# A four-stage transformer block on one core: unread products split around a branch, expert results by halves, and output pieces woven into the next stage

## The chip, the cores and the metric

The kernel runs on one core of a Trainium2 chip. The metric is the device time of one execution in microseconds (us), lower is better. The engines are named as the profile names them: PE (TensorE, matrix products), DVE (VectorE), ACT (ScalarE), POOL (GpSimd) and SP (SyncE, which here only issues DMAs).

## The reference

The inputs are `x` (4 batches of 512 tokens, 256 features, float32) and one condition vector per batch. Cut to its stages:

```python
moe  = sum over the 2 best of 8 experts: weight * (relu(relu(x@W1+b1)@W2+b2)@W3+b3)
x    = x + linear_attention(moe)         # 8 heads, blocks of 32, elu(q@proj)+1 features
c    = softmax_attention(x, condition)   # 16 heads of 16, coherence gate and field term
for layer in (0, 1):                     # local attention, 8 heads of 64, window 128
    c = c + local_attention(shift(c)) @ wo
    c = c + gated_gelu_mlp(layernorm(shift(c)))
out  = x + c
```

All arithmetic is float32. A product with 512 columns shows in the trace as two matmul records with two weight loads.

## The kernel before, in words

The program is one straight stream with one branch. Its stages follow each other, and each holds the four batches `b` as tiles of 128 tokens.

**Experts.** Each token goes to two experts. Tokens are gathered by expert into slots; each slot runs `layer`, `layer`, `last`, and `last` scatters its rows with an indirect DMA to the DRAM table `ys`. Two rare slots stand behind a runtime branch, `with tc.If(halves > NHALF - NRARE)` (L1460), which this input does not take. After the branch `busy(13)` issues 13 products of `xres[0]` that nobody reads (`pbusy`). Then, for each batch, two DMAs fetch `g` from `ys` (L1477), ACT scales the first (L1481) and DVE adds the second (L1482) into `y[b]` (`ymoe` in the trace).

**Linear attention** (`lin`). `front(b)` turns `y[b]` by PE transposes (`pt`) into `yT`, then makes `qk` and `v`. `features`, `scores` and `values` follow; `values` ends in a chain: ACT adds a small number to the sum `pz` (L1564), DVE takes its reciprocal (L1565), and DVE multiplies (L1566) into `aT`. `tail(b)` multiplies `aT` by `awo` (`pao`) and DVE adds it to `xres[b]` (L1576). One loop weaves the front of the next batch and the tail of the previous one between the products of this one.

**Conditioned attention** (`cond_stage`). `front(b)` transposes `xres[b]` into `xT2`, makes `qm` (`pcq`), `kT` (`pck`), values `v1` (`pcv`) and the gate (`pct` and small products). `attend` runs scores (`sc`), exponentials on ACT (`cex`) and values (`pv`), with fronts and tails of other batches as fill. `tail(b)` makes `yc[b]`.

**Local attention and MLP** (`local_stream`, two layers). `front` transposes `yc[b]` (`pdt`), projects it (`pdq`), and rotates q and k with DVE and POOL, with a table `tab` that DVE first scales.

**What sets the order.** Within `PE.in_order()` every PE instruction is pinned behind the one written just before it. All other instructions, on PE and on every other engine, are placed at build time by the framework's planner: it runs the program with its own costs, takes what it believes ready, and of several ready ones the one written first. So the order on DVE, ACT and POOL, and of unpinned PE work, is the planner's. At run time each engine follows its fixed list. Tiles are rotating buffers in pools; a pool that opens where another closed waits, address by address, for the last reader of the old tiles. [...] `lin` uses four for `mmt` tiles and four for `features`; `cond_stage` uses two for `mmt` (pool `ps1`) and six for scores (`sp`); `local_stream` uses all eight.

## Time and profile before

| | us |
|---|---|
| median of 3 runs | 1429.75 (1427.66 to 1430.11) |
| the profiled execution: its time | 1429.31 |
| its span, first to last instruction | 1427.5 |
| PE busy | 1354.0 (95%) |
| DVE busy | 667.0 (47%) |
| ACT busy | 586.0 (41%) |
| POOL busy | 230.4 (16%) |

The profiled execution lies 0.44 us under the median, and 1.8 us of its time lie outside the span. The granted PE clock was 0.981 of full speed over the span. The stages can be told apart by their tiles: experts up to 320.7 us, linear attention from 336.6 to 499.7, conditioned attention to 753, local attention and MLP to the end. "Idle before" names what released an engine; "issue" is a wait for nothing that the profile shows.

### The profile page before, as it was taken

The numbers are of one execution on the slowest core, as the hardware profiler recorded it, in microseconds if no ns is written. First come the engines' busy times: TensorE is split into PE (matmuls) and PEld (weight loads), VectorE is DVE, ScalarE is ACT, GpSimd is POOL, SyncE is SP. The second block draws the span as 40 slices with busy tenths as digits, with TensorE's granted clock in tenths as the row PEclk, the third lists the DMA queues.
The fourth block names the chain that finished last, engine by engine and source line by source line (L and its number), as shares of the span: only waits on it lengthen the run. The fifth ranks groups of instructions, "written<-read, shape, count | busy, mean of one in ns | idle before, by whom it ended". The sixth has DMA issues, their size and how long they took to land.

```text
span 1427.5 us, 19422 instructions
## 1 busy us (share of the span) xinstructions
PE 1354.0 (95%) x7624; PEld 835.6 (59%) x7624; DVE 667.0 (47%) x1297; ACT 586.0 (41%) x969; POOL 230.4 (16%) x219
## 2 busy tenths in 40 slices
PE   4999999998899799999999999999999999999998
PEld 3788888874566543333335555656655456556564
DVE  6222221223677642333226777754352767854331
ACT  3111111123555325554654647563222567474111
POOL 0324232111000020000102322100020312310010
PEclk8999999999999899999999999999999999999999
DMA  3577667623000000000111011211001010011000
GB/s 122 216 258 264 223 227 247 214 79 122 1 2 1 0 1 0 1 1 1 44 49 64 2 36 35 75 33 30 22 0 41 23 32 23 17 39 47 14 23 25
DMA packets 43645, 94.74 MB, mean 66 GB/s; under 512 B 9760, under 2 KB 25752, under 8 KB 40728
## 3 DMA queue, kind: packets, MB, share of 16 engines
q1 hardware_dynamic: 38984, 83.11, 17.6%
q0 software_dynamic: 3552, 9.70, 2.0%
q8 instruction: 63, 1.03, 0.3%
q10 hardware_dynamic: 1008, 0.58, 0.2%
q14 instruction: 38, 0.31, 0.1%
HBM read 84.08 MB, written 7.21 MB: 64 GB/s over the span
## 4 chain that ended last, share of the span: by engine, by line
PE 66%; DVE 5%; ACT 3%; issue 2%; DMA 1%; SPq 0%; DVEq 0%; POOL 0%; POOLq 0%
PE pdq L78 11%; PE pug L78 5%; PE sc L78 5%; PE pua L78 5%; PE pv L78 5%; PE pn L78 4%; PE pfy L78 4%; PE pdy L78 4%; PE pds L78 4%; PE pz L78 2%; PE pqt L82 2%; PE pqk L78 2%; PE pcq L78 1%; PE pur L78 1%; PE pcv L78 1%
## 5 line engine op out<-in xcount | busy, mean ns | idle before, releaser
L78 PE MATMUL pdq<-wqkv,yT 128*128 128x512 f32 x384 | 177.6, 603 | 4.5 <-ACT yT L583 4.5
L403 ACT ACTIVATE cex<-sc 128x1024 f32<-128x1024 f32 x128 | 124.1, 1021 | 95.8 <-PE sc L78 94.7
L78 PE MATMUL ph<-h,w 128*128 128x256 f32 (+1 forms) x704 | 133.4, 347 | 1.0 <-ACT h L1356 0.5
L653 DVE TENSOR_TENSOR p<-p,lmask 128x384 f32<-128x384 f32 (+1 forms) x128 | 98.4, 786 | 66.5 <-ACT p L651 65.0
L609 POOL TENSOR_TENSOR qr<-t,t 128x512 f32<-128x512 f32 x64 | 85.8, 1340 | 247.5 <-DVE t L606 229.8
L78 PEld LDWEIGHTS ph<-h,w 128*128 128x128 f32 x704 | 116.2, 191 | 13.3 <-DVE h L1358 0.7
L78 PEld LDWEIGHTS pdq<-wqkv,yT 128*128 128x128 f32 x384 | 69.5, 190 | 82.2 <-issue 72.8
L1358 DVE TENSOR_SCALAR h<-ph,w 128x256 f32<-128x256 f32 (+1 forms) x88 | 36.1, 438 | 164.5 <-PE ph L78 101.5
L1356 ACT ACTIVATE h<-ph,w 128x256 f32<-128x256 f32 (+1 forms) x88 | 35.4, 438 | 187.1 <-PE ph L78 132.5
L651 ACT ACTIVATE p<-pds,ss 128x256 f32<-128x256 f32 (+1 forms) x256 | 95.6, 457 | 35.8 <-PE pds L78 27.3
L78 PE MATMUL pug<-hT,w 128*128 128x512 f32 x160 | 78.3, 612 | 0.0
L599 ACT ACTIVATE sq<-pdq 128x512 f32<-128x512 f32 x64 | 38.3, 598 | 96.7 <-PE pdq L78 57.6
L78 PE MATMUL sc<-qm,kT 32*128 32x512 f32 x512 | 76.0, 647 | 0.0
L78 PE MATMUL pua<-hT,w 128*128 128x512 f32 x160 | 75.6, 595 | 0.0
L78 PE MATMUL pv<-cex,v 128*32 128x512 f32 x512 | 69.0, 604 | 1.7 <-DVE xT L292 1.7
L78 PE MATMUL ph<-xbT,w 128*128 128x256 f32 (+1 forms) x352 | 68.3, 346 | 0.0
L78 PE MATMUL po<-w,h 128*128 128x256 f32 x296 | 67.7, 380 | 0.5 <-ACT h L1356 0.5
L78 PE MATMUL pdy<-wo,oT 128*128 128x256 f32 x256 | 63.3, 392 | 3.3 <-DVE oT L693 3.3
L78 PE MATMUL pds<-qT,kT 64*128 64x256 f32 (+1 forms) x512 | 65.3, 375 | 0.0
L78 PEld LDWEIGHTS pds<-qT,kT 64*128 64x128 f32 x512 | 43.9, 186 | 32.9 <-issue 26.2
L78 PEld LDWEIGHTS ph<-xbT,w 128*128 128x128 f32 x352 | 58.4, 191 | 6.9 <-issue 0.9
L78 PE MATMUL pfy<-w,uA 128*128 128x256 f32 x256 | 61.2, 382 | 0.0
(294 smaller groups left out, 2103.5 us busy)
## 6 DMA issues: line engine op xcount, KB each, us to landing
w<-in_moe_w_dram SPq DMA_DIRECT2D x22, 1024.0 KB
w<-in_moe_w_dram SPq DMA_DIRECT2D x22, 640.0 KB
w<-in_moe_w_dram SPq DMA_DIRECT2D x22, 516.0 KB
zb<-rows SPq DMA_DIRECT2D x32, 256.0 KB
g<-ys SPq DMA_DIRECT2D x8, 512.0 KB
wqkv<-in_f_wqkv_dram SPq DMA_DIRECT2D x2, 1536.0 KB
w<-in_f_w_dram SPq DMA_DIRECT2D x2, 1408.0 KB
xres<-in_x_dram SPq DMA_DIRECT2D x4, 512.0 KB
```

The costliest lines, as they stand in the source:

```text
L78: cls._queue(nc.tensor.matmul(*args, **kw))
L82: cls._queue(nc.tensor.transpose(*args, **kw))
L403: nc.scalar.activation(ex, pss[j], AF.Exp, scale=CHD**-0.5)
L599: nc.scalar.activation(sq, p3, AF.Square)
L609: nc.gpsimd.tensor_tensor(qr_t[:, s], t1, t2, ALU.add)
L651: nc.scalar.activation(p[:, at], pss[r][:, at], AF.Exp, scale=d.ss[:, 2 * u + jj, 1, 2 * c + r : 2 * c + r + 1])
L653: nc.vector.tensor_tensor(p[:, :n], p[:, :n], lmask[:, :n], ALU.mult)
L1356: nc.scalar.activation(dst, src, AF.Relu, bias=bias)
L1358: nc.vector.tensor_scalar(dst, src, bias, 0.0, ALU.add, ALU.max)
```

## The change

It touches three places where one stage hands over to the next ("seams"), and moves work between them.

- **Experts to linear attention.** `busy(13)` behind the branch becomes `busy(3)` ahead of it and `busy(6)` behind it. Batch 0's results are fetched in four DMAs of half the size (two tiles of tokens each), batch 1's in two as before. Only batch 0 is summed at once; `weighted(b)` of the other batches is written at the head of their `front` in `lin`, and so are the DMAs of batches 2 and 3.
- **Linear to conditioned attention.** The last batch's `tail` is no longer run at the end of `lin`: it is handed to `cond_stage` as `before`, and its two output pieces are put, pinned, between pieces of `front(0)`: both transposes, both `pck`, then one output piece, one `pcq`, one output piece, one `pcq`. So that this works, `pck` now comes ahead of `pcq` in every `front`; batch 0's `xT2` and `kT` are written by ACT instead of DVE; `aT` of the last batch and `awo` live in the pool `wp` that stays open; the last reciprocal and product run in two halves; the score banks are allocated ahead of `ps1`; `v1` is cleared inside `front(0)` and `front(1)`.
- **Conditioned to local attention.** The first `front` of the first local layer is no longer pinned.

```diff
+    def cond_stage(W, cp, sp, safe, before=()):
...
-            v1s = []
-            for i in range(2):
-                v1 = cp.tile([128, NT, CH, 32], F32, tag=f"v1{i}", name=f"v1{i}", bufs=1)
-                nc.gpsimd.memset(v1, 0.0)
...
+        v1s = []
+
+        def make_v1():
+            i = len(v1s)
+            v1 = cp.tile([128, NT, CH, 32], F32, tag=f"v1{i}", name=f"v1{i}", bufs=1)
+            nc.gpsimd.memset(v1, 0.0)
+            nc.gpsimd.memset(v1[:, :, :, CHD : CHD + 1], 1.0)
+            v1s.append(v1)
...
-                nc.vector.tensor_copy(xT2[:, c, :], pt)
+                (nc.scalar.copy if b == 0 else nc.vector.tensor_copy)(xT2[:, c, :], pt)
...
+            if not safe and b < 2:
+                make_v1()
+            for c in range(2):
+                ps = mmt("pck")
+                mm(ps, [(W["wqkv"][:, k, H + c * 128 : H + (c + 1) * 128], xT2[:, k, :]) for k in range(2)])
+                if b == 0:
+                    nc.scalar.activation(kT[:, c, :], ps, AF.Identity, bias=col("bk", c))
+                else:
+                    nc.vector.tensor_scalar(kT[:, c, :], ps, col("bk", c), None, ALU.add)
+                yield
             for c in range(2):
                 ps = mmt("pcq")
...
-                ps = mmt("pck")
-                mm(ps, [(W["wqkv"][:, k, H + c * 128 : H + (c + 1) * 128], xT2[:, k, :]) for k in range(2)])
-                nc.vector.tensor_scalar(kT[:, c, :], ps, col("bk", c), None, ALU.add)
-                yield
...
-        run(front(0, ds[0]))
+        first = front(0, ds[0])
+        with PE.in_order():
+            for _ in range(4):
+                next(first)
+            for _ in before:
+                next(first)
+        run(first)
...
+        run(front(wa, 0, ds[0]))
         with PE.in_order():
-            run(front(wa, 0, ds[0]))
             for l in range(2):
...
-                "awo": lambda: weight("awo", [128, 2, H], chunks(a["a_woT"]), wl),
+                "awo": lambda: weight("awo", [128, 2, H], chunks(a["a_woT"]), wp),
...
             last(len(often) - 1, often[-1])
+
+            busy(3)
             with tc.If(halves > NHALF - NRARE):
...
-            busy(13)
...
-            for b in range(B):
-                gs = []
-                for k in range(2):
-                    g = gp.tile([128, NT, H], F32, tag=f"g{k}", name=f"g{k}", bufs=2)
-                    at = 1 + (k * B + b) * S
-                    nc.sync.dma_start(g, ys[at : at + S].rearrange("(t p) h -> p t h", p=128))
-                    gs.append(g)
+            busy(6)
+
+            def results(b):
+                gs = [gp.tile([128, NT, H], F32, tag=f"g{k}", name=f"g{k}", bufs=2) for k in range(2)]
+                n = 2 if b == 0 else NT
+                for t in range(0, NT, n):
+                    for k in range(2):
+                        at = 1 + (k * B + b) * S + t * 128
+                        nc.sync.dma_start(gs[k][:, t : t + n, :],
+                                          ys[at : at + n * 128].rearrange("(t p) h -> p t h", p=128))
+                return gs
+
+            def weighted(b, gs):
                 for t in range(NT):
...
+            both = {b: results(b) for b in range(2)}
+            weighted(0, both[0])
...
             def front(b, d):
+                if b:
+                    weighted(b, both[b])
+                if b + 2 < B:
+                    both[b + 2] = results(b + 2)
...
-                    d.aT = lp.tile([128, 2, S], F32, tag="aT", name="aT")
+                    pool, tag = (wp, "aTlast") if d is ds[-1] else (lp, "aT")
+                    d.aT = pool.tile([128, 2, S], F32, tag=tag, name="aT")
...
-                nc.vector.reciprocal(z, z)
-                nc.vector.tensor_tensor(d.aT[:, g, :], pn, z, ALU.mult)
+                n = S // 2 if d is ds[-1] and g == 1 else S
+                for at in range(0, S, n):
+                    half = slice(at, at + n)
+                    nc.vector.reciprocal(z[:, half], z[:, half])
+                    nc.vector.tensor_tensor(d.aT[:, g, half], pn[:, half], z[:, half], ALU.mult)
...
-            run(tail(B - 1, ds[B - 1]))
+            end = tail(B - 1, ds[B - 1])
...
+            sp = cst.enter_context(tc.tile_pool(name="sp", bufs=3, space=PSUM, reuse_waits="tile"))
             cst.enter_context(banks("ps1", mm=2))
-            sp = cst.enter_context(tc.tile_pool(name="sp", bufs=3, space=PSUM, reuse_waits="tile"))
...
-            y = cond_stage(cw_, cp, sp, False)
+            y = cond_stage(cw_, cp, sp, False, end)
```

More of the change, by code (lines that the diff above doesn't have):

```diff
@@ L271, in conditions @@
         W["csb"], W["faT"] = csb, faT
-    def cond_stage(W, cp, sp, safe):
+    def cond_stage(W, cp, sp, safe, before=()):
         csb, faT = W["csb"], W["faT"]
         y = [resp.tile([128, NT, H], F32, tag="res", name=f"yc{b}") for b in range(B)]
-        if not safe:
-            v1s = []
-            for i in range(2):
-                v1 = cp.tile([128, NT, CH, 32], F32, tag=f"v1{i}", name=f"v1{i}", bufs=1)
-                nc.gpsimd.memset(v1, 0.0)
-                nc.gpsimd.memset(v1[:, :, :, CHD : CHD + 1], 1.0)
-                v1s.append(v1)
+        v1s = []
[5 more added lines that the diff above has]
+            v1s.append(v1)
         def front(b, d):
```

## The prediction

> **What bounds the kernel now.** I read the page first (PE busy 95% of the span, granted clock 0.981), so only PE's idle time, PE's work that nobody reads, and PE at a lower clock can be won. The view of all waits of PE shows where the idle lies, and most of the long ones stand at the three seams. Busy time by stretch (columns: stretch, length, busy time and instructions of PE, weight loads, DVE, ACT, POOL; granted clock; DMA):

> ```profile
> 320.70:336.60 15.90, 12.52 (x26) 5.45 (x26) 3.77 (x9) 4.58 (x11) 1.19 (x3) 0.89 0.65 213
> 336.60:346.10 9.50, 7.12 (x20) 2.79 (x18) 5.95 (x9) 3.42 (x8) 2.57 (x1) 0.82 0.31 102
> 489.40:502.00 12.60, 7.48 (x26) 5.37 (x25) 6.18 (x6) 0.69 (x1) 2.23 (x2) 0.73 0.01 1
> 744.90:753.80 8.90, 6.36 (x38) 5.06 (x36) 4.46 (x10) 0.60 (x2) 0.23 (x2) 1.00 0.35 121
> ```

> The 12.52 us of the first row are all unread products. Three rows are also under full clock. The chain of waits at the first seam (start, length, what):

> ```profile
> 321.66 2.45 issue
> 324.11 12.23 PE pbusy L78 x24
> 336.34 0.81 ACT g L1481 x2
> ...
> 337.16 3.36 DVE ymoe L1482 x3
> ...
> 340.85 0.69 DVE yT L125
> ...
> 341.58 4.54 PE pqk L78 x6
> ```

> The timeline of the same time says that batch 0's sum is done long before the unread products end (ACT, then DVE, waiting for the DMA):

> ```profile
> 328.32 1.71 ACT L1481 ACTIVATE g<-g,m 128x256 f32<-128x256 f32 x4 [8.85 <-DMA g<-ys]
> 329.79 1.67 DVE L1482 SCALAR_TENSOR_TENSOR ymoe<-g,m,g 128x256 f32<-128x256 f32 x4 [8.59 <-DMA g<-ys]
> ```

> So `y[0]` is whole at 331.46, but its transposes stand behind `pbusy` until 337.04; then the copy of `yT`'s second half waits on DVE behind batch 2's sum. Second and third seam, from the chain:

> ```profile
> 490.19 3.37 DVE z L1565
> ...
> 494.40 5.33 PE pao L78 x12
> ...
> 500.58 0.64 PE pt L82 x4
> ```

> ```profile
> 745.73 0.67 PE pcot L82 x4
> ...
> 749.44 3.29 PE pcy L78 x14
> ...
> 753.84 17.45 PE pdq L78 x40
> ```

> At the second, PE idles 3.90 us for reciprocal and product, and the 12 output products then take 5.33 us where 8 took 1.73 earlier. At the third, PE waits in steps of 0.3 to 1.2 us for DVE copies.

> [...] after 3.4 us without products the clock is 0.50 from 325.5 to 328.5, and passes of `pbusy` come 0.855 us apart instead of 0.43; the same after the 3.90 us at 490.5 (0.53). [...] PE's record of the branch is at 320.5, its next instruction at 324.08, with no releaser.

> ```profile
> L1460 PEldq COMPARE_BRANCH x1: 358/358/358, 320.5 to 320.5; - x1
> ```

> [...] If PE's sequencer ran ahead, the branch would overlap queued products. The trace doesn't settle it: DVE's and ACT's branch records come 0.2 and 0.1 us after their last instruction's end, PE's when its last product runs.

> **First seam.** Removed: 7 of 13 unread products behind the branch net of 3 put ahead (14 passes go behind it, 6 come ahead). I take it that the branch follows the three: 320.5 + 6 x 0.43 = 323.1, plus the same 3.6 us, restart at 326.7. `busy(6)` is 12 passes: 5.2 us, or 6.2 if two us of them are at half clock; taken to 332.4. Four half-size DMAs carry the same bytes, so the last lands where batch 0's second did (329.75); only two sums of 0.48 are left: `y[0]` at 330.7, hidden under `busy(6)`. Eight transposes (1.04 us) to 333.4; ACT copies one half (0.59), DVE the other (0.68), to 334.2. Two `pqk` groups (4 passes, 1.72 us each) end at about 337.5, where before `features` began at 346.05: 8.5 us. Late next is DVE: POOL's `xres += bo` (2.57 us) waits for the last `pbusy`, since that reads `xres[0]`, and a DVE sum beside it took 2.57 us instead of 0.48 (the maximum of the L1482 row). It will now fall on batch 1's sum, which the planner may place ahead of the second `yT` copy: up to 2.5 us. I take half: **-7.5 us**. Bounds: -11 (the branch runs ahead, restart at 324.1, everything 2.6 earlier) and -5 (that, with POOL falling on batch 0's sum, or a second cold window of 1.7).

> **Sums in the next stream.** 12 ACT scalings (0.43, 5.1 us) and 12 DVE sums (0.42, 5.0 us) leave the seam. SP issues ten DMAs instead of eight (0.36 to 1.07 us each) with nothing else of its own until 707.6. Batch 2's rows can be asked for when batch 0's buffers are free (330.7), and before took 3.9 us for the first and 1.45 more for the second: there at 336, batch 3's by about 342, long before their transposes (before: past 390 and 425). From 380 to 470 DVE is busy 65.1 of 90 us and ACT 50.9, so there is room; but PE there waits 4.7 us for `f` and 3.2 for `sc`, so a sum placed ahead of these shows. **+0.5**, bounds 0 and +3.

> **Second seam.** Before, from the end of `pz` (489.36) to the first `pcv` (509.20): 19.84 us. After, PE's list is transposes 1.04, two `pck` 3.44, two `pcq` 3.44, two output pieces 3.46 at full clock: 11.4. The reciprocal (3.37, now 2 x 1.7) and product (2 x 0.36) end at 494.3 and lie under transposes and `pck`, which need only `xres[0]`, done long ago. If that cover is gone (banks or memory not free), 3.9 us of idle come back. ACT, idle for 24.5 us before its first `cT`, takes two copies (0.59) and two `kT` (0.69); the first copy costs PE 0.5. With two `mmt` banks each piece waits for the one two before: pieces of 1.72 against evacuations of 0.7 (1.6 for `qm`, which lets `pcq` and `pcv` just pass). POOL's clearing of `v1` (1.81 + 0.17) waited for `pao` because `awo` lay under it; it has 10 us now. The second one moves into a time in which POOL is idle. 19.84 - 11.9 = **-7.9**, bounds -8.4 and -5 (a DVE step late for each piece). Swapped `pck`/`pcq` in the other fronts have the same sizes: 0, bounds -1 and +1.

> **Third seam.** From 744.94 to 775.5 PE works 6.36 + 20.87 us and idles 3.3. Freed from the pin, `pdt` and `pdq` can fill these gaps, on score banks that are free after the last exponentials. What limits it: `tab` was issued at 745.40, since its memory held `v1`, and DVE scales it (1.8 us) before its first rotation; DVE's own work in this time is 23 us of 30.6. With `v1` moved and `awo`, `aT` in `wp`, `tab` may come earlier or later. **-2.4**, bounds 0 and -3.3.

> **Sum.** -7.5 + 0.5 - 7.9 - 2.4 = -17.3. Everything behind the seams is PE-bound and shifts along. Against the profiled execution, 1429.31 - 17.3 = 1412.0; that one lies 0.44 under the median, so **1412.5 us** beside the median of 1429.75. A measurement can tell about 0.2% (2.9 us) from no change.

> **Rivals.**
> - *As forecast*, 1408 to 1417: chance 0.64.
> - *The branch is overlapped.* For it: [...] a PE record of the branch while a product runs. Against: the records of DVE and ACT. The first seam gives 10 instead of 7.5, some 1409, with luck at the other seams 1406: 0.12.
> - *One seam does not do what it says.* The planner keeps the third as it was (1415), or bank or memory waits keep 3.9 us at the second (1416.5), or a sum sits ahead of the `yT` copies and PE cools again (1417), or two of these (1421). For it: batch 2's sum did sit there before. 0.17.
> - *Slower: the moved sums become a wait at each batch.* The transposes of `y[b]` are pinned, so if the planner lists a batch's sums behind the reciprocals, PE stands for 1.71 + 1.67 + 3.37 = 6.8 us, cools (1.7) and loses 8.5 three times: +25.5 - 17.8 = +7.7, 1437. It decides from 6 us per batch. Against: rows come 50 us ahead, and DVE has 25 us free of 90. 0.05.
> - *No change within 0.2%*: the same with half the wait, 0.02.

> The range, **1406 to 1421**, leaves out the last two, two seams lost at once, and the best luck. Faster 0.93, same 0.02, slower 0.05.

> **What would show it.** Right: the first `pbusy` at 320.7, 3.6 us of wait between two groups of it, the second `pbusy` starting near 326.7 and `features` near 337.5; no wait over 1 us between `pz` and `pcv` of batch 0, that stretch 12 us long and at full clock; `pdt` ahead of the last `pcy`. Wrong: `pt` of a later batch waiting on `ymoe`; a clock of 0.5 in 326 to 346; PE waiting on ACT's `xT` or `kT`; `pdq` unmoved behind `pcy`, or DVE's rotations waiting for `tab`.

## The result, and the profile after

The changed kernel takes **1415.28 us** (median of 4 runs, 1411.08 to 1417.29) against 1429.5 us for the kernel before, run beside it: ratio 0.9894, 95% interval 0.987 to 0.9918. Forecast were 1412.5 us and 1406 to 1421. The profiled execution took 1415.46 us (span 1413.7, granted clock 0.986); against the 1429.31 us of the profile before that is 13.85 us less, where the sum of the prediction had 17.3. By the medians it is 14.2 us less, so the forecast took some 3 us too many.

Busy time by stretch in the changed kernel (columns as in the prediction: stretch, length, PE, weight loads, DVE, ACT, POOL; granted clock; DMA share, GB/s). The rows answer to the four shown of before:

```profile
321.30:332.50 11.20, 8.35 (x21) 3.36 (x19) 1.81 (x5) 1.82 (x4) 3.52 (x4) 1.00 0.55 178
332.50:339.10 6.60, 6.26 (x16) 2.76 (x16) 2.74 (x6) 3.84 (x9) 0.00 (x0) 0.74 0.81 249
480.70:492.70 12.00, 11.76 (x42) 7.03 (x42) 8.07 (x10) 3.03 (x5) 2.07 (x3) 1.00 0.01 1
727.90:736.90 9.00, 6.24 (x35) 4.99 (x36) 4.61 (x10) 0.59 (x1) 0.00 (x0) 1.00 0.05 7
```

The third row is the second seam: 12.6 us with 7.48 busy at clock 0.73 have become 12.0 with 11.76 busy at full clock, and sixteen more PE instructions are in it. The fourth row is the third seam, and nearly the row of before. The first seam is shorter, but its second part still runs at 0.74.

PE's timeline at the first seam (start, length, what; in brackets the idle time before and who ended it):

```profile
319.72 1.67 PE L78 MATMUL po<-w,h 128*128 128x256 f32 x7
321.24 2.74 PE L78 MATMUL pbusy<-xres,ident 128*128 128x512 f32 x6
324.27 5.39 PE L78 MATMUL pbusy<-xres,ident 128*128 128x512 f32 x12 [0.30 <-PEq L1476]
329.50 0.46 PE L82 MATMUL pt<-ident,ymoe 128*128 128x128 f32 x2
332.53 1.21 PE L82 MATMUL pt<-ident,ymoe 128*128 128x128 f32 x6 [2.58 <-DVE ymoe L1501]
333.98 5.15 PE L78 MATMUL pqk<-yT,awqkv 128*128 128x512 f32 x8 [0.23 <-ACT yT L123]
339.06 1.98 PE L78 MATMUL pf<-qk,aproj 32*128 32x512 f32 x8
```

and DVE's sums of batch 0 in the same time:

```profile
328.69 0.88 DVE L1501 SCALAR_TENSOR_TENSOR ymoe<-g,m,g 128x256 f32<-128x256 f32 x2 [6.83 <-DMA g<-ys]
331.99 0.88 DVE L1501 SCALAR_TENSOR_TENSOR ymoe<-g,m,g 128x256 f32<-128x256 f32 x2 [2.43 <-DMA g<-ys]
```

Two things differ from the forecast. PE is back 0.30 us after the six passes ahead of the branch, where before it stood for 3.38. Its record of the branch is at 321.2 us, as they begin; a packet of the instruction queue q8 (0.02 MB) lies between 322.7 and 323.7 us, while they run, and before one lay between 321.5 and 322.7, while PE stood. That PE waited for this packet, a fetch of what follows the branch, is inferred from these times. And the second halves of batch 0's rows land at 331.97, so PE stands for 2.58 us with its unread products used up, and then runs `pqk` in part at half clock (5.15 us for what takes 3.70 at full clock in a run below). PE's timeline at the second and at the third seam, and DVE's first use of `tab`:

```profile
480.71 1.09 PE L82 MATMUL pt<-ident,xres 128*128 128x128 f32 x8
482.04 3.70 PE L78 MATMUL pck<-xT,cwqkv 128*128 128x512 f32 x8 [0.24 <-ACT xT L294]
485.58 1.89 PE L78 MATMUL pao<-awo,aT 128*128 128x256 f32 x8
487.31 1.88 PE L78 MATMUL pcq<-xT,cwqkv 128*128 128x512 f32 x4
489.02 1.89 PE L78 MATMUL pao<-awo,aT 128*128 128x256 f32 x8
490.81 1.98 PE L78 MATMUL pcq<-xT,cwqkv 128*128 128x512 f32 x4
492.63 2.70 PE L78 MATMUL pcv<-cwqkv,xT 128*128 128x256 f32 x11
```

```profile
730.98 0.63 PE L82 MATMUL pt<-ident,cat 128*128 128x128 f32 x4 [1.21 <-DVE cat L450]
731.45 0.60 PE L78 MATMUL pcy<-cwout,caT 128*128 128x256 f32 x2
732.39 3.29 PE L78 MATMUL pcy<-cwout,caT 128*128 128x256 f32 x14 [0.35 <-DVE caT L512]
735.52 0.60 PE L82 MATMUL pdt<-ident,yc 128*128 128x128 f32 x4
736.54 0.66 PE L82 MATMUL pdt<-ident,yc 128*128 128x128 f32 x4 [0.42 <-DVE yc L520]
737.03 20.91 PE L78 MATMUL pdq<-wqkv,yT 128*128 128x512 f32 x48
```

```profile
736.40 0.42 DVE L573 TENSOR_TENSOR tab<-tab,drows 128x256 f32<-128x256 f32 x1
```

The second seam is what was drawn: output pieces between the layer's products, one wait of 0.24 us. At the third, `pdt` still stands behind the last `pcy`, with all the waits, and `tab` is scaled behind them, although it was asked for at 692.0 instead of 745.4.

Times between landmarks, in us, each measured from the end or the start of an instruction of PE:

| stretch | before | after |
|---|---|---|
| end of the last expert product (`po`) to the first `pf` (the first product of `features`) | 25.32 | 17.66 |
| on to the end of the last `pz` | 143.4 | 141.7 |
| on to the first `pcv` | 19.77 | 11.85 |
| end of the last `pv` to the first `pqt` (the first transpose of the rotated q) | 30.58 | 30.87 |
| from there to the end of the span | 651.93 | 654.94 |

(The prediction's 19.84 for the third row takes 489.36, the start of the next product, as the end of `pz`.) Part of each gain is clock. In the first three rows the granted clock drops to 0.50 for 3.41 us or for two such windows on end (6.83), and each window takes at most half its length, 1.71 us. The first row has two of them before and one after, the second three and two, the third two and none.

### The profile page after: what moved, and what is told of

The parts are those of the page before. It is cut to its first block, busy times and chain, and to the rows that moved or that the text cites. A ratio compares the mean times of both kernels' runs of the same rounds, so it can differ in the third digit from the quotient of the medians.

```text
span 1413.7 us, 19421 instructions
## 1 busy us (share of the span) xinstructions
PE 1346.1 (95%) x7616; PEld 831.9 (59%) x7616; DVE 662.2 (47%) x1295; ACT 587.4 (42%) x973; POOL 229.5 (16%) x219
## 4 chain that ended last, share of the span: by engine, by line
PE 65%; DVE 5%; ACT 3%; DMA 2%; issue 1%; SPq 0%; DVEq 0%; POOL 0%; POOLq 0%
PE pdq L78 12%; PE pug L78 5%; PE pua L78 5%; PE sc L78 5%; PE pv L78 5%; PE pn L78 4%; PE pfy L78 4%; PE pdy L78 4%; PE pds L78 4%; PE pz L78 2%; PE pqt L82 2%; PE pqk L78 2%; PE pck L78 1%; PE pur L78 1%; PE pcq L78 1%
## 5 line engine op out<-in xcount | busy, mean ns | idle before, releaser
L78 PE MATMUL pdq<-wqkv,yT 128*128 128x512 f32 x384 | 181.1, 613 | 4.3 <-ACT yT L597 4.3
L78 PE MATMUL ph<-h,w 128*128 128x256 f32 (+1 forms) x704 | 133.4, 347 | 0.9 <-ACT h L1370 0.5
L78 PEld LDWEIGHTS ph<-h,w 128*128 128x128 f32 x704 | 116.2, 191 | 13.2 <-ACT h L1370 0.7
L78 PEld LDWEIGHTS pdq<-wqkv,yT 128*128 128x128 f32 x384 | 70.6, 193 | 84.1 <-issue 75.7
L78 PE MATMUL pug<-hT,w 128*128 128x512 f32 x160 | 77.3, 606 | 0.0
L78 PE MATMUL sc<-qm,kT 32*128 32x512 f32 x512 | 75.4, 640 | 0.0
L78 PE MATMUL pua<-hT,w 128*128 128x512 f32 x160 | 75.2, 592 | 0.0
L78 PE MATMUL pv<-cex,v 128*32 128x512 f32 x512 | 69.0, 604 | 1.9 <-DVE xT L294 1.9
L78 PE MATMUL ph<-xbT,w 128*128 128x256 f32 (+1 forms) x352 | 69.4, 351 | 0.0
L78 PE MATMUL po<-w,h 128*128 128x256 f32 x296 | 67.7, 380 | 0.5 <-ACT h L1370 0.5
L78 PE MATMUL pdy<-wo,oT 128*128 128x256 f32 x256 | 63.3, 392 | 3.8 <-DVE oT L707 3.8
L78 PE MATMUL pds<-qT,kT 64*128 64x256 f32 (+1 forms) x512 | 65.3, 375 | 0.0
L78 PEld LDWEIGHTS ph<-xbT,w 128*128 128x128 f32 x352 | 59.5, 195 | 7.4 <-issue 1.4
L78 PEld LDWEIGHTS pds<-qT,kT 64*128 64x128 f32 x512 | 43.9, 186 | 33.0 <-issue 26.6
L78 PE MATMUL pfy<-w,uA 128*128 128x256 f32 x256 | 61.2, 382 | 0.0
```

The costliest lines, as they stand in the source:

```text
L78: cls._queue(nc.tensor.matmul(*args, **kw))
```

## The experiments

Each ratio is to the kernel before on the same chip, so ratios can be compared across the groups of runs; medians in us only within one group. Times at a seam are from the one profiled execution of each run.

**The seams one at a time.**

```diff
 # first seam alone: before.py with busy(3), busy(6), results(), weighted() as changed
 # second seam alone: after.py with
-            busy(3)
-            busy(6)
+            busy(13)
-                n = 2 if b == 0 else NT
+                n = NT
 # and all four batches fetched and summed at the seam
```

> The kernel before with the edits of the first seam alone (3 products ahead of the branch, 6 behind it, batch 0's rows by halves, other sums in the next stream); output pieces, order of pck and pcq, v1 and the local front as before. Theory (the gains of the seams add up): from the last expert product to the first product of features 17.7 us instead of 25.3, from pz's end to the first pcv still about 19.8 us; total 1422.5 us, 1420 to 1425. Rival (a stall taken away at one seam comes back as a stretch at half clock or a wait further on): over 1426. Second rival (the sums in the stream cost PE time): later fronts wait on ymoe, and the shift between features and pz shrinks by over 1 us.

> The changed kernel with the first seam as in the kernel before (13 products behind the branch, rows whole, all sums at the seam). Theory: first seam again 25.3 us from the last expert product to features, the second 11.9 us instead of 19.8 from pz's end to the first pcv; total 1421.5 us, 1419 to 1424. Rival: the second seam's gain in the changed kernel was the luck of running at full clock there, so that the stretch takes 13.5 or more here and the total is 1424 to 1427.

First seam alone: 1423.45 us, ratio 0.9956 (0.9941 to 0.9971), that is -6.3 us (-8.4 to -4.1). Second alone: 1422.25, ratio 0.9949 (0.9935 to 0.9962), -7.3 us (-9.3 to -5.4). Together that is 13.6 of the 15.2 us that the ratio of the change gives (11.7 to 18.6): within these intervals the gains add. In the second run the stretch from `pz` to `pcv` is 11.85 us, as in the changed kernel, so its rival falls. But its first seam took 23.35 us and not the 25.3 expected, with the old edits in it: it has one window at half clock there where the profile of before has two, which is nearly the whole difference. In the first run the first seam took 19.23 us and not 17.7: PE waited 3.12 us for `ymoe`, and two windows at half clock followed instead of one.

**Batch 0's rows whole; no products ahead of the branch.**

```diff
-                n = 2 if b == 0 else NT      # rows whole
+                n = NT
```
```diff
-            busy(3)                          # no split: all nine behind the branch
-            busy(6)
+            busy(9)
```

> The changed kernel with batch 0's rows fetched whole, as before. In the changed kernel the last half landed at 331.97 and PE waited 2.6 us for the sum and then ran 3.4 us at half clock. Theory (the halves themselves are late: the two last are issued at 326.1 and 326.6 instead of 325.4, and share the engines with batch 1's): the second whole fetch lands near 330.4, PE waits about 1 us, no half clock there, total 1 to 3 us under the changed kernel, 1412.5 to 1414.5. Rival (what delays batch 0 is batch 1's rows on the same engines, however batch 0 is cut): last landing at 331 to 332, wait for ymoe 2 us or more, total as the changed kernel within 1.5 us.

> The changed kernel with all 9 unread products behind the branch. Theory (the 6 passes ahead run while the branch is fetched): PE stands 3.3 to 3.7 us from the last expert product, then 18 passes of 0.43, of which some at half clock, end at 333 to 335; PE then waits under 1 us for batch 0's sum; features begin 1 to 3 us later than in the changed kernel; total 1416 to 1418.5. Rival (the branch follows the three products, so that they only move the stall): the restart behind the branch is at the same distance from the stall's begin but features come 2.6 us sooner, total 1412 to 1413.

Whole rows: 1415.92 us, ratio 0.9914 (0.9886 to 0.9943). They land earlier, at 330.4, but nothing is won: forecast were 1 us of waiting and full clock, and PE waited 2.85 us and ran one window at half clock. DVE's timeline of this run:

```profile
330.41 3.13 DVE L1501 SCALAR_TENSOR_TENSOR ymoe<-g,m,g 128x256 f32<-128x256 f32 x4 [8.56 <-DMA g<-ys]
```

and POOL's:

```profile
329.74 2.33 POOL L1522 TENSOR_TENSOR xres<-xres,crows 128x1024 f32<-128x1024 f32 x1 [5.00 <-PE pbusy L78]
```

Four sums of 0.48 us took 3.13: the first one took 1.95 and ended at 332.36, 0.29 us after POOL's addition (332.07). That is the collision that the prediction placed on batch 1's sum and of which it took half. No split: 1417.23, ratio 0.9916 (0.9887 to 0.9944). PE's timeline:

```profile
325.00 9.66 PE L78 MATMUL pbusy<-xres,ident 128*128 128x512 f32 x18 [3.66 <-issue]
334.50 1.04 PE L82 MATMUL pt<-ident,ymoe 128*128 128x128 f32 x8
```

Without products ahead of it the branch costs 3.66 us of an empty PE and a window at half clock, and `pf` comes 20.0 us after the last expert product instead of 17.66. But 1.63 us of that is a wait for `yT`, whose copy stood behind a sum that POOL held up. With six passes ahead the branch cost 0.30. The theory holds, and the prediction's assumption that the branch follows the products falls. In the total, neither run can be told from the changed kernel: the intervals overlap widely.

This leaves a rival that no run settles. No run only takes 13 unread products down to 9. The runs without the split, with whole rows, and (below) with all sums at the seam each undo one of the other parts and lose nothing that their totals resolve. So the fewer unread products may carry most of this seam's gain: before, `y[0]` was whole at 331.46 us and PE was busy with them until 337.04.

**The first seam mended.** The next kernels have the unread products read the constant rows, so that POOL's addition no longer waits for them. Two of them, called covered, also have more of these products, to keep PE busy until `y[0]` is whole, and write out the order on DVE and ACT.

```diff
-            busy(3)
+            busy(3, cw_["rows"])
-            busy(6)
+            busy(6, cw_["rows"])     # 9 (rows whole) and 10 (halves) in the covered runs
 # covered runs: tc.keep_in_program_order on the sums of batches 0 and 1 and on batch 0's copies of yT;
 # batch 1's sums are written behind these copies
```

> Batch 0's rows whole, as in the run before this, and the unread products around the branch read the constant rows instead of xres[0], so that POOL's addition of bo to xres[0] (2.33 us) no longer waits for their end and goes far ahead, among the experts. Theory (in the whole-rows run the earlier landing was eaten by POOL's addition beside batch 0's sums, which took 3.13 us instead of 1.67): the sums take 1.7 us again and end near 332.1, the transposes of batch 0 start there instead of 332.5, features begin 0.4 to 1 us before those of the changed kernel; PE still waits 2.4 us and cools; total 1413 to 1415.5. Rival (another thing slows the sums): they take about 3.1 us again, total as before it.

> As the run with the constant rows, with 9 unread products behind the branch instead of 6, and the order of the seam written out for DVE and ACT (batch 0's sums, the copies of yT, then batch 1's sums). Theory (PE's wait for batch 0 cools it, and only the cooling is lost): 18 passes end near 332.0, the sums near 332.1, no wait over 0.3 us from 324.3 to features, full clock, features near 337.2 instead of 339.06; total 1.5 to 3.5 us under the changed kernel, 1411.5 to 1414. Rival (the half-clock stretches come from load, not from the waits; one taken away here appears elsewhere): features earlier by 1 us or so, total within 1 us of the changed kernel.

> As the covered run, with batch 0's rows by halves and 10 unread products behind the branch. Theory (halves make the last rows land 1 to 1.5 us later than whole rows): 20 passes end near 332.9, batch 0's sums near 332.9, features near 338.0, between the changed kernel and the covered run with whole rows; total 1412.5 to 1415. Rival (halves cost nothing once POOL is out of the way): batch 0's sums end by 332.2 and PE then stands behind the unread products, not behind the sums.

Constant rows, whole: the sums take 1.67 us again with POOL's additions far ahead (they start from 131.2 to 138.2 us), so the slowdown was POOL's.

```profile
330.10 1.67 DVE L1502 SCALAR_TENSOR_TENSOR ymoe<-g,m,g 128x256 f32<-128x256 f32 x4 [8.90 <-DMA g<-ys]
```

The time did not follow: 1416.61 us, ratio 0.9901 (0.9878 to 0.9924), `pf` came 19.2 us after the last expert product and not earlier than the 17.66 of the change, since PE waited 1.74 us and this time ran two windows at half clock and not one, over nearly all of `pqk` (6.12 us). The forecast of this run missed there. The covered runs do what they should at the seam: `pf` after 16.12 us with whole rows and 16.48 with halves, instead of 17.66. PE's timeline with halves has no wait for `ymoe`, and `pqk` at full clock:

```profile
324.12 8.82 PE L78 MATMUL pbusy<-crows,ident 128*128 128x512 f32 x20 [0.30 <-PEq L1479]
332.78 1.04 PE L82 MATMUL pt<-ident,ymoe 128*128 128x128 f32 x8
334.10 3.70 PE L78 MATMUL pqk<-yT,awqkv 128*128 128x512 f32 x8 [0.28 <-ACT yT L123]
337.73 1.13 PE L78 MATMUL pf<-qk,aproj 32*128 32x512 f32 x4
339.92 1.13 PE L78 MATMUL pf<-qk,aproj 32*128 32x512 f32 x4 [1.06 <-DVE qk L125]
```

The last line shows where most of the 1.2 to 1.5 us went: the second `pf` now waits 1.06 us for DVE's copy of `qk`, which the planner put behind three of batch 2's sums. With whole rows a window at half clock also follows this wait, as the rival of that run had it. Totals are 1415.5 us, ratio 0.9891 (0.9868 to 0.9914), with whole rows and 1412.91, ratio 0.9886 (0.9865 to 0.9906), with halves: neither can be told from the change, where the forecast with whole rows was a gain of 1.5 to 3.5 us. In the run with halves its rival is right: the sums end at 331.67, and PE stands behind the unread products. Over all profiles, without POOL beside the sums, batch 0 is whole 6.9 to 7.3 us after its first fetch is issued when fetched whole (4 runs), and 6.7 to 8.6 us with halves (5 runs). Halves brought nothing forward that these few executions show.

**The sums written at the seam again.**

```diff
-            both = {b: results(b) for b in range(2)}
-            weighted(0, both[0])
+            for b in range(B):
+                weighted(b, results(b))
```

> The changed kernel with all four batches' fetches and sums written at the seam as in the kernel before, the rest of the change kept. The order on PE, POOL and SP is that of the changed kernel; on DVE and ACT only one sum of batch 3 has another place. Theory (the planner puts the sums where it likes, writing them in the next stream does nothing): total within 1.5 us of the changed kernel, no clear change between features and pz. Rival (the sums in the stream are what shortened the time from features to pz): that time is longer by 1 us or more.

1413.53 us, ratio 0.9884 (0.9865 to 0.9902). From `pf` to `pz` it took 144.88 us against 141.72, which is what the rival asks for; yet the last run below, which has the changed kernel's own instructions in the same order, took 144.74. The difference is clock: both have four windows at half clock in this stretch, the profile of the change two and before three. With half of PE's busy time at half clock taken off, the stretch is 138.4 us before, 138.4 in the change, 138.2 here and 138.0 in the last run. So the rival falls, and moving the sums cost and won nothing here within 0.5 us.

**The third seam.** (The first expectation calls the conditioned attention "convolution-attention".) First a control that gives the last tail's inputs other memory, so that it can be written inside the local stage; then the weave itself; then the weave with the covered first seam; and last the changed kernel with the front pinned again.

```diff
 # control: batch 3's cat and cwout in the memory of w2, its fterm in yc, caT in a buffer of qT
+            run(end)
+            run(front(wa, 0, ds[0]))
 # woven: instead
+            nxt = front(wa, 0, ds[0])
+            next(nxt); next(end); next(nxt); next(end); next(nxt)
+            for _ in end:
+                next(nxt)
+            run(nxt)
 # pinned again
-        run(front(wa, 0, ds[0]))
         with PE.in_order():
+            run(front(wa, 0, ds[0]))
```

> The changed kernel with another place for what the last tail of the convolution-attention stage reads: batch 3's cat and cwout lie in the memory of w2, its fterm in yc itself, its caT in a local buffer, so that this tail can be written inside the local stage. The order on PE is that of the changed kernel (tail, then pdt, then pdq). It is the control of the next run. Theory: from the end of the last pv to the first pqt 30.9 us as in the changed kernel (within 0.4), total 1413.5 to 1417. Rival (the other places cost a wait or bring a load forward): that time changes by over 0.5 us.

> As the control, with the local stage's first pieces written out between the pieces of the last tail: pdt, pt, pdt, pt, pdq, half of pcy, pdq, the other half of pcy, then the rest of pdq. This is what the third seam's edit was taken to do. Theory (PE's waits of 2.8 us at this seam can be filled, and tab is scaled on DVE 4 us sooner): from the end of the last pv to the first pqt 27.6 to 28.9 us, 2 to 3.3 less than in the control. Rival (DVE's own work of some 23 us sets the time to pqt, so that PE only waits later): less than 1 us gained.

> The woven third seam together with the covered first seam with halves (10 unread products behind the branch, which read the constant rows, order of the sums written out). Theory (the gains add): first seam 16.5 us from the last expert product to features, second 11.9 us, third 28 us; total 2 to 5 us under the changed kernel, 1410 to 1413. Rival (what is gained comes back as half-clock stretches): total within 1.5 us of the changed kernel.

> The changed kernel with the local stage's first front pinned again, as before: it comes out with the same list of instructions on every engine as the changed kernel. It measures what two builds of one program differ by. Theory (the third seam's edit does nothing): total within 1.5 us of the changed kernel's 1415.3, each stretch between landmarks the same but for half-clock stretches of 3.4 us (1.7 us lost each), which may lie elsewhere. Rival (the edit has an effect that the lists don't show): from the last pv to the first pqt another time by over 0.5 us at the same clock.

From the last `pv` to the first `pqt`: 31.77 us in the control, **27.59** woven, 27.60 woven with the covered seam, 30.86 pinned again. The control's rival is right: a reduction came ahead of `tab`'s scaling on DVE, and the first `pqt` waited 2.52 us for `qr`. PE's timeline of the woven kernel, where two short waits are left:

```profile
731.12 0.66 PE L82 MATMUL pcot<-ident,co 128*128 128x128 f32 x4 [0.79 <-DVE co L427]
731.61 0.60 PE L82 MATMUL pdt<-ident,yc 128*128 128x128 f32 x4
732.05 0.60 PE L82 MATMUL pt<-ident,keep 128*128 128x128 f32 x4
732.88 0.63 PE L82 MATMUL pdt<-ident,yc 128*128 128x128 f32 x4 [0.24 <-DVE keep L454]
733.35 0.60 PE L82 MATMUL pt<-ident,keep 128*128 128x128 f32 x4
733.78 1.88 PE L78 MATMUL pdq<-wqkv,yT 128*128 128x512 f32 x4
735.50 1.89 PE L78 MATMUL pcy<-keep,caT 128*128 128x256 f32 x8
```

Its DVE scales `tab` at 734.60, ahead of its first rotation, which is 4.3 us after the end of the last `pv` and not 8.5 as in the changed kernel:

```profile
734.60 0.41 DVE L579 TENSOR_TENSOR tab<-tab,drows 128x256 f32<-128x256 f32 x1
736.34 0.69 DVE L620 TENSOR_REDUCE ss<-sq 128x8 f32<-128x512 f32 x1 [0.18 <-ACT sq L619]
736.94 0.68 DVE L622 TENSOR_TENSOR t<-pdq,tab 128x512 f32<-128x512 f32 x1
```

Totals: control 1417.23 us, ratio 0.991 (0.9895 to 0.9925); woven **1410.13**, ratio 0.9862 (0.9843 to 0.988); with the covered seam 1412.2, ratio 0.9871 (0.9856 to 0.9886); pinned again 1413.36, ratio 0.9887 (0.9872 to 0.9902). Against its control the woven kernel is clearly faster. Its place explains 4.2 us of the 7.1 between the medians; in the profiled executions another 2.6 lie behind `pqt`, where the control has more windows at half clock. Against the changed kernel's program on the same chip it is 3.2 us faster by the medians, which is its 3.3 us between the landmarks, but the intervals overlap a little. It has the lowest ratio of all. That the two mended seams add up is not shown: with both, the ratio is no better than with the weave alone. The covered seam won 0.86 us at its place (16.50 against 17.36) and again lost 1.06 in the second `pf`.

## Why the prediction was right, and where it was wrong

The two seams that carry most of the forecast gave what it said, and so the total fell into its range. That it fell so close is in part luck, since errors cancelled in the first seam and clock windows moved other stretches both ways. Two of its own signs of being wrong did appear: a clock of 0.5 between 326 and 346 us (333.5 to 336.9), and `pdq` unmoved behind `pcy`.

**First seam** (-7.5, measured -7.66 in the profile, -6.3 alone): the sum was right by luck, for two terms were wrong and cancelled. (By its own terms, 8.5 less half of 2.5, it should also have read -7.25.) The step "the branch follows the three" failed: PE was back at 324.27, not 326.7, although the experts before it ended 0.66 us later. This was the rival of the overlapped branch, for which PE's record of the branch, while a product ran, had spoken; without the split `pf` came 2.3 us later, 1.6 of it behind another wait. The step "`y[0]` at 330.7" failed as well: 332.87. The prediction let the last half land where the whole second row had landed (329.75); the halves landed 2.2 us later, 0.7 of it from the experts. So `busy(6)` ended before it, and 2.58 us of waiting and a loss of 1.6 us by a window at half clock came back. For POOL's addition beside the sums the prediction took half of 2.5 us. In this execution it fell between the two pairs of sums and cost nothing. In the whole-rows run it cost 1.5 us of DVE; in the run pinned again, the same program as the change, the third sum took 1.35 us for 0.48.

**Sums in the next stream** (+0.5, measured -1.6): the price should have been nothing. What was measured is one window at half clock less; with that loss taken off, the stretch is 138.4 us before and after. PE's, POOL's and SP's order is the same wherever the sums are written.

**Second seam** (-7.9, measured -7.9; alone -7.3): right in each step. Reciprocals and products lay under transposes and `pck`, the pieces came every 1.7 us, ACT's first copy cost PE 0.24 and not 0.5. Some 2.5 of the 7.9 us are clock: before, PE worked for 5.0 us in two windows at half clock around the wait of 3.90 us, which are gone.

**Third seam** (-2.4, measured +0.3): the step that failed is "freed from the pin, `pdt` and `pdq` can fill these gaps". Nothing asked the planner to move them, and it didn't: with the pin and without it the kernel has the same instructions in the same order on all five engines. The rival that named this put the time at 1415. The price was somewhat small for the thing itself: written out by hand it gives -3.3 against the changed kernel, the end of the bounds, and -4.2 against its control.

**"Everything behind shifts along"** (0, measured +3.0 from `pqt` to the end): the same program, run as pinned again, took 651.29 us there where the profile of the change shows 654.94 and before 651.93. The other runs lie between 650.9 and 654.8. So the loss is not shown to be the change's: ahead of the last microseconds, three windows at half clock lie in it in the one execution (767, 1101 and 1309 us) and one in the other. With half of PE's busy time at half clock taken off, the two are 649.9 and 649.6, and before 648.9; that last 1 us stays open.

The account of the 3.5 us missing from 17.3: experts +0.7, first seam -0.2, sums -2.1, second seam 0, third seam +2.7, the end +3.0, the rest of conditioned attention -0.5. The sums' share and 2 us of the end's are clock and not the change.

## What to carry to other kernels

Put unread work ahead of a branch rather than behind it: here it filled the time in which PE otherwise stood after the branch, and 3.66 us of idle PE with a half-clock window behind them became 0.30. And count how much of it is needed: with 13 products PE was still at them 5.6 us after the input was there. Taking an instruction out of a fixed order asks for nothing: compare the two instruction lists before you price it, and if the order matters write it out. When a wait is shortened, look for what moves into its place: here POOL's addition, which hung on the end of the unread products, moved onto the very sums that PE was waiting for.

## What was unexpected of the hardware

PE fell to half clock after much shorter waits than the 3.4 and 3.9 us of which the prediction tells, and not in every execution. The changed kernel's program in two executions, both times after waits of 0.65 and 1.31 us; first the profile of the change, then the run pinned again:

```profile
355.09 1.13 PE L78 MATMUL pf<-qk,aproj 32*128 32x512 f32 x4 [1.31 <-DVE f L1563]
356.14 1.98 PE L78 MATMUL pqk<-yT,awqkv 128*128 128x512 f32 x4
```

```profile
353.58 1.13 PE L78 MATMUL pf<-qk,aproj 32*128 32x512 f32 x4 [1.31 <-DVE f L1563]
354.64 3.10 PE L78 MATMUL pqk<-yT,awqkv 128*128 128x512 f32 x4
```

```profile
350.58:354.00 3.42, 2.55 (x17) 1.48 (x16) 2.63 (x4) 3.27 (x5) 0.00 (x0) 1.00 0.00 0
354.00:357.41 3.41, 2.32 (x7) 1.01 (x8) 2.76 (x3) 3.03 (x4) 0.00 (x0) 1.00 0.02 5
```

```profile
351.96:355.37 3.41, 2.10 (x8) 0.81 (x7) 2.98 (x4) 2.92 (x4) 0.00 (x0) 1.00 0.02 5
355.37:358.78 3.41, 3.41 (x9) 1.92 (x8) 1.54 (x2) 2.04 (x3) 0.00 (x0) 0.50 0.00 0
```

In the first the grid cuts the wait of 1.31 us in two, and PE is busy for 75% and 68% of the two windows. In the second this wait lies in one window, PE is busy for 62% of it, and the next window runs at half clock. Over all traces, from 50 us on, all 46 windows at full clock in which PE was busy for less than 42% were followed by half clock, and none of the 5222 with more than 75%; of the 178 between, 36 were. So what counted in these traces was how busy PE was in a window of the grid, and not the length of one wait; what decides between 42% and 75% stays open.

No window without any work was needed: the one ahead of the half clock was 62% busy here, and at the restart that the prediction cites PE was busy for 1.21 us of the window from 321.91 to 325.32. Since the half-clock windows differ between executions of one program, one execution of this kernel can't show a gain of under about 3 us in the total, however exact its timeline is: from `pqt` to the end alone the two executions lie 3.65 us apart (654.94 and 651.29), and the four runs of the changed kernel 6.2 us.

POOL's addition did not slow DVE's sums down, it held one of them up. In each of the 8 traces where a sum began beside the addition with 0.6 us or more of it still to run, that sum ended 0.28 us after the addition (before: 340.14 and 339.86), so that it took from 0.89 to 2.58 us. A sum that had begun just ahead of the addition took its usual 0.48 us.
